# A two-layer graph network on one core: all heads scaled by ScalarE, the last list decode spread out, weights loaded earlier

## The chip, the core and the metric

The kernel runs on one core of one Trainium2 chip. The metric is the device time of one execution in microseconds. Three runs of the kernel before took 671.46, 673.04 and 673.52 us; the median is 673.04 us. One more execution was profiled: 674.27 us, of which the profile's span, from the first to the last instruction, is 672.6 us.

## The reference, cut to what matters

```python
x, adj: 4096 x 512 floats, 4096 x 4096 ints (about 4 ones in a row)
# layer 0: graph attention, 8 heads of 64, W: (8, 512, 64), a: (8, 128)
Wh = einsum('nf,hfo->hno', x, W)
e  = leaky_relu(f1[:, :, None] + f2[:, None, :], 0.2)     # f1, f2: Wh against the halves of a
attn = softmax(where(adj > 0, e, -9e15), axis=-1)
x  = layernorm(x + concat_heads(attn @ Wh))
# layer 1: mean of the neighbours and the node itself
agg = (adj > 0) @ x / max(deg, 1)
y  = relu(concat([x @ W_self + b_self, agg @ W_nb + b_nb]) @ W_comb + b_comb)
out = layernorm(x + y)
```

## The kernel before, in words

The rows are handled in 32 blocks of 128 (`NB = 32`). There are three stages. The order of instructions on each engine is the order in which the program issues them (`tc.manual_schedule()`); no scheduler moves them. Waits are added where data or a buffer require them.

**Stage 1, reading adj.** For each block two halves of 128x2048 ints are loaded by SP's DMA queue (`load_adj`, L413, four buffers `at`), turned to bf16 by ScalarE with a row sum (`mask_adj`, L419, three buffers `ab`), folded by TensorE into keys (`fold_adj`, L437), and the largest keys are taken by VectorE (`max_keys`, L452). Beside it TensorE computes Wh (`node_half`, L367), which goes to a table `t0` in DRAM. After every fourth block, `decode` turns the keys of four blocks into neighbour lists. It is a generator: each `next` runs one piece on VectorE (sometimes with a small matmul), 16 pieces for four blocks. Pieces 4 to 7 each search one block's list; pieces 9 and 10 are empty; pieces 11 to 14 build selection matrices; 15 has the matmuls L517; 16 fills `own`.

**Hand-over.** After the last block, the weights of layer 1's neighbour half are loaded (`load_fold`, `wr` and `wc`, L276 and L277, 1 MB each on SP's queue) and multiplied together on TensorE (`fold_weights`, a generator of 16 pieces: four chunks, each with transposes L293, a ScalarE copy L294, four matmuls L305 and a ScalarE copy L309). GpSimd starts the gathers: each block of layer 0 needs five indirect DMAs (`gather`, L612) of table rows. The second gather buffer lies where the adj buffers were (`ap_cm.__exit__`), so block 1's gathers wait until the last `mask_adj` has read its buffer.

**Stage 2, attention.** A software pipeline over steps i = -3 to 33. In step i, in this order:

- TensorE: `a_shared(i+1)` (L696), `a_z(i-1)` (L744), transposes of block i (L346)
- VectorE: `a_weights(i+3)` (L645), `a_weigh(i+2)` (L662), `a_recip(i+1)` (L704), `a_first`, `a_own_sum`, `a_adds(i+2)` (L670 to L686), the last part of `a_scale(i+1)` (L715), then one list piece (`some(lists)`), then `a_moments(i+1)` (L722), in some steps a bias piece (`fold_bias`, L324)
- ScalarE: `root(i)` (L730 to L736) and `norm(i)` (L739), `a_scale(i+1)` (L712), `a_exp(i+3)` (L652, L653), `a_owners(i+4)` (L639), the copy of z (L748), the copy of xT (L352)
- GpSimd: five gathers for block i+6, as soon as `a_shared(i+1)` frees the buffer (five buffers, `GA = 5`)

`a_scale` multiplies the eight heads' sums in PSUM by the reciprocals: `HA = 6` heads as six ScalarE instructions of 128x64 and the last two as one VectorE instruction of 128x128. `root(i)` needs the result of `a_moments(i)`, and `a_moments(i+1)` needs all of `a_scale(i+1)`.

The last decode (blocks 28 to 31) runs its pieces in steps 0 to 15, one in each; `late_lists` (five pieces, L555 to L597, for rows that layer 1 gathers late) follows in steps 17 to 21; bias pieces run in steps 2 to 5 and 16 to 19; `sum_bias` (L332, L333) in step 20; step 7 loads 2 MB of weights on SP's queue.

**Stage 3, layer 1.** For each block TensorE does `g_shared` (L783) and `g_self` (L776); GpSimd gathers five sets of rows per block from table `t1`, which `a_z` filled; the result goes out.

Of the kernel before, what the change touches and what calls it, by code (L numbers as in the profile page):

```python
# [36 lines left out]
OP = mybir.AluOpType  # L37
# [3 lines left out]
P = 128  # L41
# [71 lines left out]
def listed_layers(  # L113
# [15 lines left out]
    nc = tc.nc  # L129
    N, FIN = x.shape  # L130
    H, _, D = w0.shape
    NB = N // P
    FB = FIN // P
    HD = H * D
    HH = HD // 2
# [12 lines left out]
    FIRST = (0, 1, 3)  # L148
    EARLY = NB - 3
    LB = NB - 2  # L150
    HA = 6

    t0 = tc.dram_tile([N + 2, TW], F32, name="t0")
    t1 = tc.dram_tile([N + 2, HD], F32, name="t1")
# [111 lines left out]
    def pads(wp):  # L266
        pad = wp.tile([P, FW], F32, name="row", bufs=2)
        nc.vector.memset(pad[0:1, 0:H], -BIG)
        nc.vector.memset(pad[0:1, H:FW], 0.0)
        nc.scalar.dma_start(t0[0:1, :], pad[0:1, 0:TW])  # L270
        nc.scalar.dma_start(t1[0:1, :], pad[0:1, H:TW])
        nc.scalar.dma_start(t1[1:2, :], pad[0:1, H:TW])


    def load_fold(k, w, wr, wc):
        nc.sync.dma_start(wr, w.rearrange("(c p) o -> p c o", p=P))  # L276
        nc.sync.dma_start(  # L277
            wc, w_comb[k * HD : (k + 1) * HD, :].rearrange("(c p) o -> p c o", p=P)
        )
        return wr, wc  # L280
# [9 lines left out]
    def turned(wr, c, wT, bank):  # L290
        tp = ps.tile([P, FB, P], F32, name=bank)
        for d in range(FB):
            nc.tensor.transpose(tp[:, d, :], wr[:, c, ts(d, P)], ident)  # L293
        nc.scalar.copy(wT, tp.rearrange("p c r -> p (c r)"))  # L294
        return wT.rearrange("p (c r) -> p c r", c=FB)

    def fold_weights(loaded, place, bank):

        wr, wc = loaded
        wT = turned(wr, 0, place(0), bank)  # L300
        for c in range(FB):
            nxt = turned(wr, c + 1, place(c + 1), bank) if c + 1 < FB else None
            mp = ps.tile([P, HD], F32, name="mp")
            for d in range(FB):
                nc.tensor.matmul(  # L305
                    mp, lhsT=wT[:, d, :], rhs=wc[:, d, :], start=(d == 0), stop=(d == FB - 1)
                )
                if d == FB - 1:
                    nc.scalar.copy(wr[:, c, :], mp)  # L309
                yield  # L310
            wT = nxt
# [24 lines left out]
    def load_x(b, eng=nc.sync):  # L336
        if b < NB:
            eng.dma_start(xs[:, b, :], x[ts(b, P), :])
# [69 lines left out]
    def load_adj(b, ap):  # L408

        for h in range(NH):  # L410
            at = loads[b, h] = ap.tile([P, NG // NH, SC], I32, name="at", bufs=4)
            r = b * P + h * (P // NH)
            nc.sync.dma_start(  # L413
                at, adj[r : r + P // NH, :].rearrange("(j r) (s c) -> (r s) j c", r=RG, s=SEG)
            )

    def mask_adj(b, h):
        ab = masks[b, h] = bp.tile([P, NG // NH, SC], BF16, name="ab", bufs=3)
        nc.scalar.activation(  # L419
            ab, loads.pop((b, h)), AF.Relu, accum_out=asum[:, b, h : h + 1]  # L420
        )
# [189 lines left out]
    def rows_of(out, table, at):  # L611
        nc.gpsimd.indirect_dma_start(  # L612
            out=out, out_offset=None, in_=table,
            in_offset=bass.IndirectOffsetOnAxis(ap=at, axis=0),
        )
# [5 lines left out]
    def gather(table, b, g, at=None):  # L621
        for k in range(KS):
            rows_of(
                g[:, k, 0 : table.shape[1]], table, (idx if at is None else at)[:, b, k : k + 1]
            )
        return g
# [8 lines left out]
    G0, OWN, E, RD, Y, NM, MV, RS = ({} for _ in range(8))  # L635

    def a_owners(b, wp):
        OWN[b] = wp.tile([P, KH, P], F32, name="own", bufs=4)
        nc.scalar.copy(  # L639
            OWN[b].rearrange("p k c -> p (k c)"), own[:, b].rearrange("p k c -> p (k c)")  # L640
        )
# [63 lines left out]

    def a_scale(b):

        for h in range(HA):
            a, q = divmod(h, H // 2)
            o = a * HD + (1 - a) * H + q * D  # L710
            s = NM[b][:, o : o + D]
            nc.scalar.mul(s, s, RD[b][:, h : h + 1])  # L712
        o = HD + HH - (H - HA) * D
        s = NM[b][:, o : HD + HH].rearrange("p (h d) -> p h d", d=D)
        nc.vector.tensor_tensor(  # L715
            s, s, RD[b][:, HA:].unsqueeze(2).to_broadcast([P, H - HA, D]), OP.mult
        )

    def a_moments(b, wp):
        Y[b] = wp.tile([P, HD], F32, name="y", bufs=2)  # L720
# [95 lines left out]
    def some(todo):  # L816
        for p in todo:
            next(p, None)

    wp = ctx.enter_context(tc.tile_pool(name="work", bufs=1))  # L820
    fc_cm = tc.tile_pool(name="foldc", bufs=1, side="right")
    fc = fc_cm.__enter__()
    fp_cm = tc.tile_pool(name="fold", bufs=1, side="right")
    fp = fp_cm.__enter__()

    def weight(pool, name):
        return pool.tile([P, FB, HD], F32, name=name)
# [101 lines left out]
    for b in range(LB - 1):  # L929
        for k in range(1 + (b in AHEAD)):  # L930
            load_x(w + k + XL)
        load_adj(b + 2, ap)
        if b == 4:
            pads(wp)
        for k in range(2):
            some(lists)
        for k in range(1 + (b in AHEAD)):
            nxt = transposed(w + 1, wp, sums)
            if k == 0 and b in (22, 23, 24):
                transposed(EARLY + b - 22, wp, sums, True)  # L940
            if k == 0:
                key_bank(b + 1)
                for h in range(NH):
                    mask_adj(b + 1, h)
            node_block(w, xT, None if k else b)
            w, xT = w + 1, nxt
        for k in range(2):
            some(lists)
        if b == 25:
            pieces = mean_row(w_sb, sums, xa)  # L950
        if b >= 25:
            next(pieces, None)
        if b % G == G - 1:
            lists = [decode(b + 1 - G, dp, on_own)]
    m2 = weight(fp, "wr")
    loaded = load_fold(1, w_nb, m2, weight(fc, "wc"))
    load_adj(LB + 1, ap)
    row = node_block(w, xT, keep=True)
    key_bank(LB)
    mask_adj(LB, 0)  # L960
    store(w, row)
    fold_adj(LB - 1, dp)
    max_keys(LB - 1)
# [3 lines left out]
    def place(c):  # L967
        return wp.tile([P, FW], F32, name="row", bufs=2)[:, 0:FIN]
# [4 lines left out]
    def pieces(n, todo):  # L973
        for k in range(n):
            next(todo)

    gps = [gather_buffer(0)]
    G0[0] = gather(t0, 0, gps[0])
    mask_adj(LB, 1)
    key_bank(LB + 1)  # L980
    m2s = fold_weights(loaded, place2, "pw")
    pieces(1, m2s)
    fold_adj(LB, dp)
    max_keys(LB)
    pieces(3, m2s)
    mask_adj(LB + 1, 0)
    for k in range(4):
        some(lists)
    pieces(3, m2s)
    mask_adj(LB + 1, 1)  # L990
    pieces(1, m2s)
    ap_cm.__exit__(None, None, None)
    gps.append(gather_buffer(1))
    G0[1] = gather(t0, 1, gps[1])
# [14 lines left out]
                t[:, a * HD : (a + 1) * HD], lhsT=triu, rhs=cols, start=True, stop=True  # L1009
            )  # L1010
    G0[2] = gather(t0, 2, gps[2])
    a_owners(0, wp)
    lists = [chain(lists[0], decode(NB - G, dp, on_last))]


    def on(b):
        return 0 <= b < NB
# [3 lines left out]
    for i in range(-3, NB + 2):  # L1021
        if on(i + 1):
            a_shared(i + 1)
        if on(i + 1 + GA):
            G0[i + 1 + GA] = gather(t0, i + 1 + GA, gps[(i + 1 + GA) % GA])
        elif on(i + GA - NB - 1) and i + GA - NB - 1 < GA:
            b = i + GA - NB - 1
            G1[b] = gather_early(b, gps[(NB + b) % GA])
        if on(i + 3):
            a_weights(i + 3, wq)  # L1030
        if on(i + 2):
            a_weigh(i + 2, slice(K0, KS))
        if on(i + 1):
            a_recip(i + 1, wq)
        if on(i + 2):
            a_first(i + 2)
            a_weigh(i + 2, slice(1, K0))
            a_own_sum(i + 2)
            a_adds(i + 2)
        if on(i):  # L1040
            root(i, xs[:, i, :])
            norm(i, xs[:, i, :])
        if on(i + 1):
            a_scale(i + 1)
        if i > -3:
            some(lists)
        if i == 16:
            lists = [late_lists(dp, last.rearrange("p g (a k) -> p (g a) k", a=2))]
        if on(i + 1):
            a_moments(i + 1, wq)  # L1050
        if on(i + 3):
            a_exp(i + 3)
        pieces({-3: 2, -2: 2}.get(i, 0), m2s)
        if on(i + 4) or i == -3:
            a_owners(i + 4, wp)
        if on(i - 1):
            a_z(i - 1, XT.pop(i - 1), m2, wp)
        if on(i):
            XT[i] = transposed(i, wp)
            store_xT(i, XT[i])  # L1060
        if 2 <= i < 6:
            next(biased)
        if i == 7:
            loaded = load_fold(0, w_self, m1, weight(fc, "wc"))
        if 16 <= i < 20:
            if i == 16:
                biased = fold_bias(loaded, bcol[:, 0:FB])
            next(biased)
        if i == 20:
            sum_bias()  # L1070
# [481 lines left out]
```

## Time and profile before

| what | us |
|---|---|
| median of three runs | 673.04 |
| the profiled execution, time | 674.27 |
| its span | 672.6 |
| TensorE busy (share of the span) | 597.7 (89%) |
| VectorE busy | 472.4 (70%) |
| ScalarE busy | 476.6 (71%) |
| GpSimd busy | 352.6 (52%) |
| stage 1, until the last row of t0 is stored | 0 to 220 |
| hand-over, until root(0) starts | 220 to 254.4 |
| stage 2, root(0) to root(31) | 254.4 to 462.2 |
| stage 3, from the first L783 | 472.2 to 672.6 |

In a timeline line the columns are the start and the duration in us, the engine, the line of the kernel, the operation with its tiles and shapes, how many were merged, and in brackets how long the engine stood idle before it and what ended that. In a table of stages, each line is one stretch of time: its bounds, its length, then the busy time and the number of instructions of PE, PEld, VectorE (DVE), ScalarE (ACT) and GpSimd (POOL), the granted TensorE clock, the DMA share and GB/s.

### The profile page before, as it was taken

To read this page: it belongs to the slowest core of one execution; us is meant where nothing else is said; L and a number is where in the kernel's file an instruction comes from. 1 tells how busy PE (TensorE), PEld (TensorE's weight loads), DVE (VectorE), ACT (ScalarE), POOL (GpSimd) and SP (SyncE) were. 2 spreads that over 40 slices of the span, in tenths; PEclk is the share of its full clock that TensorE was granted. 3 is DMA by queue.
4 is the path that set the end of the run, shared out by engine and by line. 5 is a ranking of instruction groups with operands and counts; after the bars stand their busy time and mean duration, and the time that the engine had idled before them with its cause. 6 is when DMAs were issued, how large, how long until landed. Compare 5 with 4: busy or idle time off the path is not lost.

```text
span 672.6 us, 8973 instructions
## 1 busy us (share of the span) xinstructions
PE 597.7 (89%) x2229; PEld 346.2 (51%) x2230; DVE 472.4 (70%) x1293; ACT 476.6 (71%) x1249; POOL 352.6 (52%) x474
## 2 busy tenths in 40 slices
PE   4788989898798958978899889999899999999993
PEld 2566767666665335545455456564444444444441
DVE  6236867868786569999899999992315665666663
ACT  2688888788886326888788778996326677677664
POOL 5111111111112577777777756547777677777760
PEclk9988989989999876999999999999999999999997
DMA  8999999999999577989998987859879898999991
GB/s 247 408 408 407 409 407 408 407 410 408 402 405 405 182 210 229 290 287 298 391 283 299 281 260 224 297 183 295 284 221 307 255 329 310 307 317 308 312 310 67
DMA packets 92037, 209.63 MB, mean 312 GB/s; under 512 B 13694, under 2 KB 13702, under 8 KB 91978
## 3 DMA queue, kind: packets, MB, share of 16 engines
q1 hardware_dynamic: 63024, 114.05, 45.3%
q0 software_dynamic: 28624, 94.39, 43.9%
q10 hardware_dynamic: 330, 0.54, 0.3%
q8 instruction: 20, 0.33, 0.2%
q14 instruction: 39, 0.32, 0.2%
HBM read 175.25 MB, written 33.69 MB: 311 GB/s over the span
## 4 chain that ended last, share of the span: by engine, by line
PE 51%; DMA 26%; DVE 8%; ACT 7%; issue 3%; POOL 3%; SPq 1%; ACTq 0%; DVEq 0%; POOLq 0%
DMA at<-in_adj_dram 15%; PE nm L776 8%; PE pw L776 8%; PE pw L744 8%; DMA g<-t,idx 8%; PE pw L367 6%; PE num L696 5%; PE nm L783 4%; PE pw L783 4%; ACT ab L419 4%; PE tp L305 3%; POOL g L612 3%; DMA wc<-in_L_gnn_W_comb_dram 2%; DVE g L662 2%; PE tp L346 2%
## 5 line engine op out<-in xcount | busy, mean ns | idle before, releaser
L612 POOL DMA_INDIRECT g<-t,idx x290 | 276.1, 952 | 106.9 <-issue 37.5
L419 ACT ACTIVATE ab<-at 128x2048 bf16<-128x2048 int32 x64 | 122.5, 1915 | 32.4 <-DMA at<-in_adj_dram 26.7
L367 PE MATMUL pw<-w_sb,xT 128*128 128x264 f32 x512 | 135.2, 411 | 8.1 <-issue 3.8
L744 PE MATMUL pw<-wr,xT 128*128 128x512 f32 x256 | 116.5, 598 | 3.2 <-ACT xT L352 3.2
L367 PEld LDWEIGHTS pw<-w_sb,xT 128*128 128x128 f32 x512 | 97.2, 199 | 37.0 <-issue 7.2
L374 POOL COPY lst<-row 128x8 f32<-128x8 f32 x32 | 6.5, 203 | 165.0 <-DVE row L371 152.2
L696 PE MATMUL num<-g,own 128*128 128x264 f32 (+1 forms) x256 | 71.7, 429 | 18.7 <-DVE num L686 10.2
L662 DVE TENSOR_TENSOR g<-g,ew 128x1024 f32<-128x1024 f32 x64 | 77.4, 1210 | 0.0
L744 PEld LDWEIGHTS pw<-wr,xT 128*128 128x128 f32 x256 | 48.5, 192 | 52.2 <-issue 46.2
L696 PEld LDWEIGHTS num<-g,own 128*128 128x128 f32 x256 | 51.2, 210 | 32.5 <-DVE num L686 12.8
L712 ACT ACTIVATE num<-num,rd 128x64 f32<-128x64 f32 x192 | 54.7, 285 | 10.0 <-DVE rd L704 4.8
L776 PE MATMUL nm<-m,xT 128*128 128x512 f32 x128 | 57.5, 592 | 0.0
L776 PE MATMUL pw<-m,xT 128*128 128x512 f32 x128 | 57.5, 592 | 0.0
L371 DVE COPY row<-pw 128x264 f32<-128x264 f32 x64 | 27.3, 426 | 33.4 <-PE pw L367 21.4
L799 DVE SCALAR_TENSOR_TENSOR sm<-y,lst,nm 128x512 f32<-128x512 f32 x16 | 12.1, 754 | 52.4 <-PE nm L793 28.7
L346 PEld LDWEIGHTS tp<-ident,xs 128*128 128x128 f32 x256 | 32.2, 148 | 29.5 <-issue 11.5
L686 DVE TENSOR_TENSOR num<-num,g 128x512 f32<-128x512 f32 x64 | 44.7, 699 | 2.2
L346 PE MATMUL tp<-ident,xs 128*128 128x128 f32 x256 | 41.1, 285 | 5.7 <-DVE tl L570 2.5
L776 PEld LDWEIGHTS nm<-m,xT 128*128 128x128 f32 x128 | 24.3, 190 | 30.6 <-issue 30.6
L776 PEld LDWEIGHTS pw<-m,xT 128*128 128x128 f32 x128 | 24.3, 190 | 30.6 <-issue 30.1
L612 POOL DMA_INDIRECT g<-t,idxe x30 | 28.5, 949 | 19.6 <-DVE num L670 9.1
L730 ACT ACTIVATE xs<-y,ln_sum 128x512 f32<-128x512 f32 x32 | 23.3, 728 | 17.1 <-DVE y L722 17.1
(219 smaller groups left out, 981.1 us busy)
## 6 DMA issues: line engine op xcount, KB each, us to landing
at<-in_adj_dram SPq DMA_DIRECT2D x64, 1024.0 KB, 10.7
xt<-xT SPq DMA_DIRECT2D x32, 256.0 KB, 4.3
t<-row SPq DMA_DIRECT2D x32, 256.0 KB, 3.9
xT<-xt SPq DMA_DIRECT2D x32, 256.0 KB, 5.1
out_dram<-row SPq DMA_DIRECT2D x32, 256.0 KB, 5.5
t<-row POOLq DMA_DIRECT2D x31, 260.0 KB, 5.5
xs<-in_x_dram SPq DMA_DIRECT2D x31, 256.0 KB, 10.7
g<-t,idx POOLq DMA_INDIRECT x290, 5.0
```

The source lines that it names most:

```text
L346: nc.tensor.transpose(tp[:, c, :], xs[:, b, ts(c, P)], ident)
L367: nc.tensor.matmul(pw, lhsT=xT[:, c, :], rhs=w_sb[:, c, k * HW : (k + 1) * HW], start=(c == 0), stop=(c == FB - 1),)
L371: nc.vector.tensor_copy(row[:, k * HW : (k + 1) * HW], pw)
L419: nc.scalar.activation(ab, loads.pop((b, h)), AF.Relu, accum_out=asum[:, b, h : h + 1])
L612: nc.gpsimd.indirect_dma_start(out=out, out_offset=None, in_=table, in_offset=bass.IndirectOffsetOnAxis(ap=at, axis=0),)
L662: nc.vector.tensor_tensor(gv, gv, E[b][:, sl].unsqueeze(3).to_broadcast([P, sl.stop - sl.start, H, D]), OP.mult,)
L686: nc.vector.tensor_add(halves_of(NM[b]), halves_of(NM[b]), G0[b][:, k, H:TW].rearrange("p (a c) -> p a c", a=2),)
L696: nc.tensor.matmul(NM[b][:, a * HD : a * HD + r.stop - r.start], lhsT=OWN[b][:, k, :], rhs=G0[b][:, K0 + k, r], start=False, stop=(k == KH ...
L712: nc.scalar.mul(s, s, RD[b][:, h : h + 1])
L744: nc.tensor.matmul(pz, lhsT=xT[:, c, :], rhs=m2[:, c, :], start=(c == 0), stop=(c == FB - 1))
L776: nc.tensor.matmul(NM[b], lhsT=xT[:, c, :], rhs=m1[:, c, :], start=False, stop=(c == FB - 1), skip_group_check=True,)
L783: nc.tensor.matmul(NM[b], lhsT=OWN[b][:, k, :], rhs=g[:, K0 + k, 0:HD], start=False, stop=(k == KH - 1), skip_group_check=True,)
```

## The change

`a_scale` does all eight heads on ScalarE; the VectorE instruction L715 and `HA` go. The last decode's pieces run in three of four steps (0, 1, 2, 4, 5, 6, 8, ... 18, 20) and `late_lists` follows in steps 22, 24, 25, 26 and 28. The two loads of `load_fold(1, ...)` are issued ahead of block 30's adj loads instead of ahead of block 31's. In the hand-over, the pieces of `fold_weights` come ahead of the masks that they used to follow: two chunks are done around the masks of block 30 and the first mask of block 31, and the last four pieces all come in step -3. The first `a_owners` moves into step -3, behind `a_exp(0)`.

```diff
-    HA = 6
@@ a_scale
-        for h in range(HA):
+        for h in range(H):
             a, q = divmod(h, H // 2)
             o = a * HD + (1 - a) * H + q * D
             s = NM[b][:, o : o + D]
             nc.scalar.mul(s, s, RD[b][:, h : h + 1])
-        o = HD + HH - (H - HA) * D
-        s = NM[b][:, o : HD + HH].rearrange("p (h d) -> p h d", d=D)
-        nc.vector.tensor_tensor(
-            s, s, RD[b][:, HA:].unsqueeze(2).to_broadcast([P, H - HA, D]), OP.mult
-        )
@@ stage 1
+        if b == LB - 2:
+            m2 = weight(fp, "wr")
+            loaded = load_fold(1, w_nb, m2, weight(fc, "wc"))
         load_adj(b + 2, ap)
...
-    m2 = weight(fp, "wr")
-    loaded = load_fold(1, w_nb, m2, weight(fc, "wc"))
     load_adj(LB + 1, ap)
     row = node_block(w, xT, keep=True)
     key_bank(LB)
-    mask_adj(LB, 0)
     store(w, row)
@@ hand-over
     G0[0] = gather(t0, 0, gps[0])
+    m2s = fold_weights(loaded, place2, "pw")
+    pieces(1, m2s)
+    mask_adj(LB, 0)
+    pieces(3, m2s)
     mask_adj(LB, 1)
     key_bank(LB + 1)
-    m2s = fold_weights(loaded, place2, "pw")
+    pieces(3, m2s)
+    mask_adj(LB + 1, 0)
     pieces(1, m2s)
     fold_adj(LB, dp)
     max_keys(LB)
-    pieces(3, m2s)
-    mask_adj(LB + 1, 0)
     for k in range(4):
         some(lists)
-    pieces(3, m2s)
     mask_adj(LB + 1, 1)
-    pieces(1, m2s)
     ap_cm.__exit__(None, None, None)
...
-    a_owners(0, wp)
@@ stage 2, step i
-        if i > -3:
+        if -3 < i < 0 or i % 4 < 3 and i >= 0:
             some(lists)
-        if i == 16:
+        if i == 21:
             lists = [late_lists(dp, last.rearrange("p g (a k) -> p (g a) k", a=2))]
...
-        pieces({-3: 2, -2: 2}.get(i, 0), m2s)
-        if on(i + 4) or i == -3:
+        if i == -3:
+            a_owners(0, wp)
+        if on(i + 4):
             a_owners(i + 4, wp)
+        if i == -3:
+            pieces(4, m2s)
```

## The prediction

> **What bounds the kernel now.** I first read the table of stages, for who is busy where in stage 2. Columns: stretch, length, busy PE, PEld, VectorE, ScalarE, GpSimd, clock, DMA share, GB/s.
>
> ```profile
> 280.00:300.00 20.00, 16.48 (x55) 9.88 (x56) 19.52 (x50) 15.63 (x49) 15.40 (x16) 1.00 0.90 289
> 360.00:380.00 20.00, 18.22 (x63) 10.59 (x62) 19.52 (x45) 16.60 (x54) 15.12 (x17) 1.00 0.91 300
> 420.00:440.00 20.00, 20.00 (x73) 12.15 (x72) 19.49 (x44) 19.05 (x63) 10.03 (x11) 1.00 0.77 257
> ```
>
> Until about 400 VectorE is full and ScalarE has a fifth free. At 420 to 440 PE, VectorE and ScalarE are all full. GpSimd looks half free, but early it issues 16 gathers in 20 us, one per 1.25 us.
>
> Next, the timeline of ScalarE over one late step, root(26) to root(27), and of VectorE: a step with a list piece, then one without.
>
> ```profile
> 428.05 0.74 ACT L730 ACTIVATE xs<-y,ln_sum 128x512 f32<-128x512 f32 x1
> 430.61 1.87 ACT L712 ACTIVATE num<-num,rd 128x64 f32<-128x64 f32 x6
> 432.41 0.20 ACT L652 ACTIVATE ew<-e 128x40 f32<-128x40 f32 x1
> 433.89 0.74 ACT L730 ACTIVATE xs<-y,ln_sum 128x512 f32<-128x512 f32 x1
> ```
> ```profile
> 302.30 0.29 DVE L715 TENSOR_TENSOR num<-num,rd 128x128 f32<-128x128 f32 x1
> 303.31 0.67 DVE L722 SCALAR_TENSOR_TENSOR y<-num,xs 128x512 f32<-128x512 f32 x1
> ...
> 427.74 0.19 DVE L645 TENSOR_TENSOR e<-g,f1s 128x40 f32<-128x40 f32 x1
> 432.60 0.29 DVE L715 TENSOR_TENSOR num<-num,rd 128x128 f32<-128x128 f32 x1
> 432.93 0.69 DVE L722 SCALAR_TENSOR_TENSOR y<-num,xs 128x512 f32<-128x512 f32 x1
> 433.54 0.20 DVE L645 TENSOR_TENSOR e<-g,f1s 128x40 f32<-128x40 f32 x1
> ```
>
> No line carries an idle bracket. ScalarE needs 433.89 - 428.05 = 5.84 us a step, six scales in 432.41 - 430.61 = 1.80 us, 0.30 each. VectorE needs 5.80, and a list piece lengthens that. PE repeats L696 at 426.95 and 432.75: 5.80 too.
>
> The waits of ScalarE from 254 to 463 tell what its free time was:
>
> ```profile
> ACT xs L730 <- DVE y L722: 17.1, 16, 2.8
> ACT row L748 <- PE pw L744: 4.8, 5, 2.3
> ACT row L748 <- PE num L696: 2.3, 1, 2.3
> ```
>
> Mostly it waited for VectorE's moments. The hand-over, last: ScalarE, PE, GpSimd and VectorE, each from its timeline.
>
> ```profile
> 225.45 0.58 ACT L309 COPY wr<-tp 128x512 f32<-128x512 f32 x1 [7.40 <-PE tp L305]
> 225.93 1.91 ACT L419 ACTIVATE ab<-at 128x2048 bf16<-128x2048 int32 x1
> 228.30 1.92 ACT L419 ACTIVATE ab<-at 128x2048 bf16<-128x2048 int32 x1
> ```
> ```profile
> 218.28 2.05 PE L305 MATMUL tp<-wc,last 128*128 128x512 f32 x2 [2.20 <-DMA wc<-in_L_gnn_W_comb_dram]
> ```
> ```profile
> 225.51 0.95 POOL L612 DMA_INDIRECT g<-t,idx  x1 [0.30 <-issue]
> 230.58 0.94 POOL L612 DMA_INDIRECT g<-t,idx  x1 [4.12 <-ACT ab L419]
> ```
> ```profile
> 240.08 0.20 DVE L645 TENSOR_TENSOR e<-g,f1s 128x40 f32<-128x40 f32 x1 [4.95 <-DMA g<-t,idx]
> ```
>
> `wc` lands at 218; PE multiplies; ScalarE stands 7.40 us behind PE with both masks of block 31 queued behind; block 1's gathers wait 4.12 us for the last mask, and VectorE 4.95 us for those gathers. That chain starts stage 2.
>
> **What the Trainium skill says.** "ScalarE: Activation LUTs", What ACT_TABLE_LOAD costs: an ACTIVATE costs 186 ns plus 0.833 ns per element plus about 93 ns per pointer operand, and neighbours overlap by some 93 ns; for 64 elements and one pointer that is 332 ns. The trace has 285 ns each and 0.30 us from one to the next, so no overlap in this chain; I use 0.30. "TensorE: Matmul & The Clock Gate", What's actually happening: after an idle window of some 3.4 us the clock halves until a busy window has passed. The trace agrees: clock 0.50 at 250 to 260, where L696 takes 3.81 us, and 1.92 later. "DMA: Bandwidth & Descriptors", Issuing engines are not separate DMA queues: all queues share 16 engines. Here they are full until 220 (share 1.05), so an earlier load only reorders landings.
>
> **Hand-over.** The 2 MB go ahead of block 30's adj. At 408 GB/s that is 5.1 us: block 30 lands at about 215.5 and 218 rather than 210.5 and 213; block 31 still lands by about 221, when the DMA share falls. `wr` and `wc` are there when PE ends the node matmuls at 214. Then on ScalarE: two L294 copies to 215.8; mask(30,0) (2.0) to 217.8; chunk 0's four matmuls (3.43) end at 218.8, L309 to 219.3; mask(30,1) to 221.3; L429 and L294 to 222.3; mask(31,0) to 224.2; L309 to 224.7; mask(31,1) to 226.7. Its buffer was mask(30,0)'s, freed by `fold_adj(30)` near 223.5, so that wait is covered. Block 0's gathers end at 226.5. Block 1's start at about 226.9: **3.7 us gained**, and G0[1], which ends VectorE's 4.95, lands 3.7 earlier. If PE falls to half clock here, the masks end at 229.8 and 0.7 is left. What hides the three extra copies and the casts of `a_owners`: VectorE waits for G0[1] anyway. Step -1 loses L715 ahead of moments(0): another 0.2. Start of stage 2: **-3.9**.
>
> **Eight scales on ScalarE.** 2 x 0.30 = 0.60 per step on an engine that has none to give late: 5.84 becomes 6.43. Over 31 steps: steps 0 to 27 give 28 x 6.43 = 180.2, less 0.5 for a missing z copy in step 0; steps 28 to 30, which drop casts and exps, 5.54, 5.37 and 5.39 plus 0.60 each, 18.1; `sum_bias`'s copy 0.5. That is 198.3 with no idle, against 207.8 measured (254.44 to 462.23) with the old load of 179.7 and so 28.1 idle. ScalarE becomes the bound; its idle decides.
>
> **VectorE.** L715 to L722 without a piece is 0.33: the step falls to 5.47. A piece costs its L715-to-L722 distance less 0.20: the search at 302.30 is 0.81; by the same reading pieces 1 to 3 are 1.05, 0.66, 0.86, piece 8 1.47, piece 11 1.17, 12 to 14 0.78, 15 1.48, 16 1.13, late pieces 1.31, 1.69, 1.31, 1.43, 1.53; a bias piece 0.66. By the new places, steps over 6.43 are: 2, 4, 5 (6.99, 6.94, 6.94), 9 (6.94), 13 (6.64), 16 to 18 (6.91, 6.91, 7.61), 20 (6.60), 22, 24 to 26, 28 (6.78, 7.16, 6.78, 6.90, 7.00). Scales end 2.56 + 2.39 = 4.95 after root, moments (0.77) by 5.7: in light steps VectorE gets up to 0.7 ahead, which swallows lone heavy steps (9, 13, 20, 22). Left: 0.6 in step 2, 0.7 in 4 and 5, 1.4 in 16 to 18, 0.8 in 24 to 26, 0.2 in 28: **3.7**. Matmuls of pieces 11 and 15 and of the late lists move with them to PE, which at 5.80 has room.
>
> **Other idle of ScalarE.** Steps 0 and 1 are paced by PE at half clock: 14.5 us stays, 2.1 over ScalarE's 12.4. Step 10 waited 3.1 (2.3, 0.8) for stores behind the 2 MB of step 7; longer steps give these more time, so between 0 and 3.1: 1.5. `sum_bias`: 1.2 as before. Sum 2.1 + 3.7 + 1.5 + 1.2 = 8.5; stage 2 takes 206.8, **-1.0**. GpSimd at 5 x 1.25 = 6.26 a step stays below 6.43. Stage 3 is PE without gaps from 509 and moves as a whole; its early gathers come sooner too.
>
> **Sum.** -3.9 - 1.0 = -4.9: 674.27 becomes 669.4 in a profiled execution; that one lies 1.2 above the median, so on the scale of the runs 673.04 - 4.9 = **668.1**. In general the shift is ScalarE's idle less 13.4.
>
> **Rivals.** (1) The hand-over yields 0.7 instead of 3.9, start and all, because PE is at half clock while ScalarE waits on its copies: -1.7, 671.3. For it: half clock at 218 to 224 before. Against: that followed PE's wait for `wc`, which goes. (2) Slower: the stalls that VectorE's bound used to hide now add to ScalarE's full queue. Place: steps 10, 16 to 28. Price: all waits of before other than on moments, 10.9, plus the heavy steps' whole excess, 6.2 to 6.7 with nothing swallowed: idle 17.1 or more, +3.7, 676.7. It decides from idle 13.4 on. For it: a wait on PE or DMA can't be made up on a full engine; against: half of the 10.9 arose where late lists, bias and `sum_bias` fell together, which the change pulls apart.
>
> **Chances.** Changes under 0.3% (2.0 us) can't be told from none. Forecast, gain over 2: 0.63. Rival 1 and idle of 11.4 to 15.4: 0.20. Rival 2: 0.17. Range: below, idle of 5 (-8.4) gives 664.6; above, it takes in rival 1 and the start of rival 2, 675.0.
>
> **What would show it.** L712 in groups of eight, 2.4 us, steps of 6.43 without brackets on ScalarE in the last third (if 5.8, the price is wrong); the wait on moments down from 17.1 to about 4; block 1's gathers at 227 (at 230: rival 1); root(0) near 250.5, root(31) near 457.4. If root(31) is past 464, rival 2.

## The result and the profile after

The changed kernel takes 672.52 us in the median of 12 runs (670.55 to 675.67); the kernel before, run beside it, 671.15 us in the median of 12 (669.11 to 673.52). The ratio is 1.001, with a 95% interval of 0.9986 to 1.0034: no difference that can be told, where 4.9 us less were forecast. In microseconds the interval reaches from -0.9 to +2.3, so the forecast gain is excluded.

The two profiled executions say something else: 674.27 us before, 671.37 after, 2.9 less. The first lies 3.1 above the median of the 12 runs of its kernel, the second 1.1 below that of its own. That gap is the main subject of what follows.

I read the profile after in the order of the prediction. The table of stages, columns as before:

```profile
280.00:300.00 20.00, 16.87 (x59) 9.99 (x58) 19.48 (x48) 17.71 (x60) 15.18 (x16) 1.00 0.92 295
360.00:380.00 20.00, 18.77 (x73) 11.06 (x73) 19.52 (x43) 18.66 (x61) 15.43 (x16) 1.00 0.93 285
420.00:440.00 20.00, 17.63 (x61) 9.96 (x61) 19.18 (x44) 18.57 (x62) 6.73 (x8) 1.00 0.55 180
```

ScalarE gained 2 us of work per 20 in the first two stretches; VectorE still looks full. Busy shares no longer tell which is the bound. The groups on the page show the moved work, with count, busy time and mean ns: 256 scales where there were 192, at 286 ns each where there were 285.

```profile
L711 ACT ACTIVATE num<-num,rd 128x64 f32<-128x64 f32 x256 | 73.1, 286 | 10.2 <-DVE rd L703 2.9
```

ScalarE's timeline, from root(26) to root(27) in the late third:

```profile
428.01 0.72 ACT L724 ACTIVATE xs<-y,ln_sum 128x512 f32<-128x512 f32 x1 [0.18 <-DVE y L716]
...
430.56 2.51 ACT L711 ACTIVATE num<-num,rd 128x64 f32<-128x64 f32 x8
432.99 0.20 ACT L651 ACTIVATE ew<-e 128x40 f32<-128x40 f32 x1
...
434.77 0.72 ACT L724 ACTIVATE xs<-y,ln_sum 128x512 f32<-128x512 f32 x1 [0.18 <-DVE y L716]
```

Eight scales take 432.99 - 430.56 = 2.43 us. This step has a late list and takes 6.76; steps without one take 6.48 where they took 5.84. The waits of ScalarE over stage 2 (254 to 463), in us, times and the longest:

```profile
ACT xs L724 <- DVE y L716: 3.4, 7, 1.4
ACT row L742 <- DMA t<-row: 2.4, 1, 2.4
ACT brow L332 <- PE tp L331: 1.2, 1, 1.2
ACT xT L351 <- DMA xt<-xT: 0.7, 1, 0.7
```

The wait for VectorE's moments fell from 17.1 to 3.4. The window is that of the prediction and opens 3.6 us behind the changed kernel's root(0), so it leaves out the wait ahead of that; from 250 to 460 the sum is 5.3. The same view of VectorE shows the other side, the kernel before first, the changed kernel second:

```profile
DVE num L715 <- ACT num L712: 5.1, 2, 3.1
```
```profile
DVE y L716 <- ACT num L711: 11.0, 9, 4.1
```

VectorE now waits for ScalarE nine times where it waited twice, and longer than ScalarE waits for it: the bound has changed hands, though not in every step. Last the hand-over, on ScalarE, GpSimd and VectorE:

```profile
219.01 0.59 ACT L308 COPY wr<-tp 128x512 f32<-128x512 f32 x1 [1.40 <-PE tp L304]
...
224.76 1.93 ACT L418 ACTIVATE ab<-at 128x2048 bf16<-128x2048 int32 x1
```
```profile
227.04 0.96 POOL L611 DMA_INDIRECT g<-t,idx  x1 [0.76 <-ACT ab L418]
```
```profile
236.34 0.20 DVE L644 TENSOR_TENSOR e<-g,f1s 128x40 f32<-128x40 f32 x1 [1.76 <-DMA g<-t,idx]
```

The 7.40 us behind TensorE became 1.40, the 4.12 of GpSimd 0.76, the 4.95 of VectorE 1.76. In this execution the hand-over is where the prediction put it: block 1's gathers at 227.04, root(0) at 250.40. Root(31) is not: 459.49 instead of 457.4.

The span can be cut in five at marks read from the timelines: the first gather of block 0 (called S from here on), root(0), root(21), root(31), the end. From root(31) to the end it takes 210.2 to 210.5 us in every kernel here but one (211.2 in e10). All profiled kernels in one table, worked out from the starts of those instructions:

```
kernel, its profile               S       S to    root(0)   root(21)
                                        root(0)   to (21)    to (31)
before                         220.39    34.05    147.56     60.23
before, another execution      220.43    33.38    148.89     59.92
after                          220.21    30.19    144.88     64.21
e1 hand-over alone             222.53    30.42    148.59     59.87
e2 eight scales alone          220.10    30.41    147.06     65.65
e3 hand-over + spread, six     222.31    29.66    145.44     63.90
e4 eight in piece steps only   221.30    30.18    144.24     63.48
e5 before + filled wait        221.99    29.70    146.39     59.07
e6 e4 + split load             220.65    30.27    139.16     63.18
e8 e6 + three fillings         222.45    30.58    139.33     63.12
e9 e6 with the old hand-over   220.60    32.13    139.91     63.20
e10 after + split load         220.46    29.31    140.96     64.20
e11 before + split load        220.51    32.94    146.05     60.02
e12 e6 + one filling           220.98    29.12    140.36     63.22
```

Each line is a single execution, and the table shows how far such a one can be trusted. Before, its other execution, e1 and e5 have the same instructions from root(0) on, and root(0) to root(31) takes 207.79, 208.81, 208.46 and 205.46 us in them.

### The profile page after: what moved, and what is told of

It is laid out like the page before. It is cut to its first block, busy times and chain, and to the rows that moved or that the text cites. A ratio compares the mean times of both kernels' runs of the same rounds, so it can differ in the third digit from the quotient of the medians.

```text
span 669.7 us, 9002 instructions
## 1 busy us (share of the span) xinstructions
PE 591.0 (88%) x2229; PEld 338.8 (51%) x2230; DVE 466.2 (70%) x1261; ACT 494.2 (74%) x1313; POOL 354.2 (53%) x474
## 4 chain that ended last, share of the span: by engine, by line
PE 42%; DMA 32%; DVE 12%; ACT 9%; issue 3%; SPq 1%; POOL 0%; ACTq 0%; DVEq 0%; POOLq 0%
DMA at<-in_adj_dram 18%; DMA g<-t,idx 10%; PE nm L770 8%; PE pw L770 8%; PE nm L777 4%; PE tp L304 4%; PE pw L366 4%; PE pw L777 4%; DVE g L661 4%; ACT ab L418 4%; PE pw L738 3%; DMA xt<-xT 2%; DVE num L685 2%; PE num L695 2%; ACT num L711 2%
## 5 line engine op out<-in xcount | busy, mean ns | idle before, releaser
L366 PE MATMUL pw<-w_sb,xT 128*128 128x264 f32 x512 | 130.4, 400 | 6.9 <-issue 3.8
L738 PE MATMUL pw<-wr,xT 128*128 128x512 f32 x256 | 119.1, 609 | 6.5 <-ACT xT L351 6.3
L366 PEld LDWEIGHTS pw<-w_sb,xT 128*128 128x128 f32 x512 | 94.6, 194 | 33.8 <-issue 9.0
L695 PE MATMUL num<-g,own 128*128 128x264 f32 (+1 forms) x256 | 66.3, 404 | 17.6 <-DVE num L685 10.3
L711 ACT ACTIVATE num<-num,rd 128x64 f32<-128x64 f32 x256 | 73.1, 286 | 10.2 <-DVE rd L703 2.9
L695 PEld LDWEIGHTS num<-g,own 128*128 128x128 f32 x256 | 47.7, 196 | 29.2 <-DVE num L685 14.4
L370 DVE COPY row<-pw 128x264 f32<-128x264 f32 x64 | 27.3, 427 | 31.9 <-PE pw L366 23.9
L770 PEld LDWEIGHTS pw<-m,xT 128*128 128x128 f32 x128 | 24.3, 190 | 30.6 <-issue 30.4
L770 PEld LDWEIGHTS nm<-m,xT 128*128 128x128 f32 x128 | 24.3, 190 | 30.6 <-issue 30.6
L777 PE MATMUL nm<-g,own 128*128 128x512 f32 x64 | 30.2, 594 | 1.3 <-ACT nm L761 1.3
```

Of the source, the lines that this page charges most:

```text
L366: nc.tensor.matmul(pw, lhsT=xT[:, c, :], rhs=w_sb[:, c, k * HW : (k + 1) * HW], start=(c == 0), stop=(c == FB - 1),)
L370: nc.vector.tensor_copy(row[:, k * HW : (k + 1) * HW], pw)
L695: nc.tensor.matmul(NM[b][:, a * HD : a * HD + r.stop - r.start], lhsT=OWN[b][:, k, :], rhs=G0[b][:, K0 + k, r], start=False, stop=(k == KH ...
L738: nc.tensor.matmul(pz, lhsT=xT[:, c, :], rhs=m2[:, c, :], start=(c == 0), stop=(c == FB - 1))
L770: nc.tensor.matmul(NM[b], lhsT=xT[:, c, :], rhs=m1[:, c, :], start=False, stop=(c == FB - 1), skip_group_check=True,)
L777: nc.tensor.matmul(NM[b], lhsT=OWN[b][:, k, :], rhs=g[:, K0 + k, 0:HD], start=False, stop=(k == KH - 1), skip_group_check=True,)
```

## The experiments

**The parts one by one.** My theory was still that of the prediction, corrected by the trace: the hand-over gives 4 us, the scales and the spread take some back. The first kernel has the hand-over part of the diff and nothing else.

```diff
 (the kernel before, with these parts of the change only)
+        if b == LB - 2:
+            m2 = weight(fp, "wr")
+            loaded = load_fold(1, w_nb, m2, weight(fc, "wc"))
...
+        if i == -3:
+            a_owners(0, wp)
...
```

> The kernel before with the hand-over part alone (loads of wr and wc ahead of block 30's adj, products ahead of the masks, a_owners(0) and the last four pieces in step -3); six heads on ScalarE, lists in the old steps. My theory: root(0) starts at about 250.5 rather than 254.4, and since stage 2 is as before (207.8 us from root(0) to root(31), step 5.84) the whole gain of about 4 us reaches the end: ratio 0.994. Rival A (the gain at root(0) is eaten in stage 2 by waits on DMA or gathers): root(0) at 250.5, but stage 2 at 210 or more and a ratio of 0.998 to 1.000. Rival B (the profiled execution of before was late in this place by chance, the gain is not real): root(0) is early here too, but the runs stand at 1.000.

Measured: 672.26 us (14 runs, 667.66 to 673.52) against 670.94; ratio 0.9998, 0.9974 to 1.0023. Here and below the ratio and its 95% interval are those on record; they are not the quotient of the two medians, which would be 1.002 here and also lies in the interval. Root(0) was at 252.95, not 250.5, because S came 2.1 later, and the median shows no gain: rival B's reading, and the first blow to my theory. The second kernel holds only the scales.

```diff
-    HA = 6
+    HA = 8
...
-        nc.vector.tensor_tensor(
-            s, s, RD[b][:, HA:].unsqueeze(2).to_broadcast([P, H - HA, D]), OP.mult
-        )
```

> The kernel before with eight heads on ScalarE alone; hand-over and list steps as before. My theory: root(0) at about 254; ScalarE's step is 6.48 us where nothing holds it, pieces in every one of steps 0 to 15 make VectorE's steps longer than that (5.47 plus 0.6 to 1.5 with two more in steps 2 to 5 and 16 to 19), so that less is swallowed than in the changed kernel, and the steps from 22 to 28 lose 0.64 each: stage 2 takes 209 to 212 us, ratio 1.003 to 1.006. Rival (VectorE's relief of 0.33 a step pays in the early half what ScalarE loses in the late half): stage 2 at 207 to 208, ratio 1.000.

Measured: 678.05 us (7 runs, 675.36 to 680.06); ratio 1.0102, 1.0067 to 1.0138. Worse than I expected, 7 us slower; the profile, taken on the fastest of the seven, shows 4.9 of them in stage 2, and the rest is not explained. Root(21) to root(31) took 65.65 against 60.23: 5.4 us, eight steps or so by 0.64. The early steps gave only 0.5 back (147.06 against 147.56), since a step now takes the longer of 6.48 on ScalarE and VectorE's with its piece. VectorE's waits of stage 2 show who is the bound:

```profile
DVE y L717 <- ACT num L712: 15.3, 13, 4.6
```

And it gave a surprise: with the old hand-over, S to root(0) took 30.41 here, as short as the new one. Third, the changed kernel with six scales:

```diff
 (the changed kernel)
+    HA = 6
-        for h in range(H):
+        for h in range(HA):
...
+        nc.vector.tensor_tensor(
+            s, s, RD[b][:, HA:].unsqueeze(2).to_broadcast([P, H - HA, D]), OP.mult
+        )
```

> The changed kernel with HA = 6 again: hand-over and spread lists, the last two heads on VectorE. My theory: ScalarE's step is 5.84 again and VectorE's 5.80 plus its pieces, of which the sum over the stage is the same as before; the gain is the hand-over's alone, root(31) about 4 us earlier than before, ratio 0.994. Rival A (spreading the pieces into the late third, where TensorE has no room at 5.80 a step, costs by itself): stage 2 at 210 us or more and a ratio of 0.998 to 1.001, as the changed kernel. If ratio 0.994, the eight scales are what took the hand-over's gain back.

Measured: 671.56 us (14 runs); ratio 1.0006, 0.9978 to 1.0034. Not 0.994, so the eight scales are not what ate the gain. It is the ratio of rival A, with stage 2 at 209.34, just short of its 210. Spreading alone (e1 to e3) shortens the early part by 3.2 and lengthens the late one by 4.0: with six scales the late list pieces are only moved. With eight (e2 to after) it saves 2.2 early and 1.4 late. Fourth, eight scales only where VectorE has a piece:

```diff
-        for h in range(H):
+        i = b - 1
+        ha = H if i < 0 or i % 4 < 3 and i < 29 else H - 2
+        for h in range(ha):
...
```

> The changed kernel with eight heads on ScalarE only in steps in which VectorE has a list piece (three of four up to step 28), and six in the others (3, 7, 11, 15, 19, 23, 27, 29 to 31). My theory: ten steps fall from 6.48 to 5.84, 6.4 us, but VectorE gets no further ahead in them, so that the excess of heavy steps is swallowed less (up to 2.5 us back): stage 2 at 204 to 206, ratio 0.993 to 0.996. Rival (light steps only let ScalarE wait for VectorE's backlog): stage 2 at 208 to 209, ratio 0.999 to 1.002, as the changed kernel.

Measured: 669.34 us (22 runs); ratio 0.9978, 0.996 to 0.9997. A small gain, less than I expected: stage 2 took 207.72, 1.4 under the changed kernel in one profile each. Light steps did fall to 5.83, but the steps behind them grew (step 28 from 6.36 to 7.01, step 24 from 6.54 to 7.21), as the rival says: VectorE no longer gets ahead in the light ones.

**Where the hand-over's gain came from.** Why is the old hand-over 34.05 once and 30.41 once? TensorE's timelines say it, the kernel with eight scales alone (e2) first, then another execution of the kernel before (e7), for which this was expected:

> The kernel before once more, for a second look at its own hand-over. Theory (half clock by chance): from the first gather to root(0) it takes 30.4 us if L305 runs at full clock after wc (six matmuls in 2.8 us), or 34 if at half (4.2 us), and all else is within 0.5 us. Stage 2 at 207.5 to 208.7. Rival: 34 us with L305 at full clock.

```profile
218.03 1.10 PE L305 MATMUL tp<-wc,last 128*128 128x512 f32 x2 [2.20 <-DMA wc<-in_L_gnn_W_comb_dram]
219.06 0.62 PE L437 MATMUL key<-ab,fold 128*32 128x512 bf16 x8
219.60 2.84 PE L305 MATMUL tp<-wc,last 128*128 128x512 f32 x6
```
```profile
218.67 1.10 PE L305 MATMUL tp<-wc,last 128*128 128x512 f32 x2 [2.37 <-DMA wc<-in_L_gnn_W_comb_dram]
219.70 1.03 PE L437 MATMUL key<-ab,fold 128*32 128x512 bf16 x8
220.66 4.08 PE L305 MATMUL tp<-wc,last 128*128 128x512 f32 x6
```

It took 674.62 us in one run, S to root(0) 33.38. The same six products behind the same wait of 2.2 to 2.4 us take 2.84 us or 4.08. The granted clock from 221 to 223 is 1.00 in the first and 0.50 in the second, so most of the six ran at half clock there. In the first profile of before even the two ahead of them took 2.05, and the six 4.19:

```profile
221.23 4.19 PE L305 MATMUL tp<-wc,last 128*128 128x512 f32 x6
```

From the first of these products to the end of the six it is 4.4 us in e2, 6.0 to 6.1 in e7, e9 and e11, and 7.1 in before. So 2.7 of the 3.6 us between before and e2 are this clock. The rest lies between block 1's gathers and root(0), where all the profiles vary from 22.4 to 23.9 us, with either order. The Trainium skill, "TensorE: Matmul & The Clock Gate", What's actually happening, says that the activity window is free-running and that the moment of the switch depends on where in it the work falls; that agrees with what is seen, though no run here shows the window itself. The prediction reckoned with an idle window of some 3.4 us, and these waits are shorter: the half clock came behind a single wait of 2.2 us (ahead of which stood 1.06 us of matmuls and another wait of 0.9), and at 245 in the kernel before behind one of 2.95. If the wait sets it off, filling the wait must make the old order as fast as the new:

```diff
             mp = ps.tile([P, HD], F32, name="mp")
+            if c == 0 and bank == "pw":
+                for _ in range(8):
+                    nc.tensor.matmul(mp, lhsT=triu, rhs=cols, start=True, stop=True)
```

> The kernel before with one addition: eight matmuls of 128x512 bf16 (0.26 us each at full clock) into mp, overwritten afterwards, in TensorE's queue where it stood 2.20 us waiting for wc. What the traces showed so far: with the old hand-over, from the first gather of block 0 to root(0) took 34.05 us in the profile of before, where the products behind that wait ran at half clock, and 30.41 us in the profile with only eight scales added, where they ran at full clock; with the new hand-over 29.7 to 30.4. Theory (revised): the 3.7 to 4 us that the hand-over part seemed to gain were TensorE's half clock in one execution, which starts or does not start behind a 2 us wait by chance. With the wait filled the span from the first gather to root(0) is 30.2 to 30.6 here, L309's first copy waits under 5 us, and the median moves by 0 to -1.5 us (the 3.6 us times how often it happens): ratio 0.998 to 1.000. Rival (the new order itself shortens the chain, and the eight scales run was the odd one): 34 us here, ratio 1.000 or above.

```profile
216.82 1.89 PE L306 MATMUL tp<-cols,triu 128*128 128x512 bf16 x8
219.21 1.13 PE L308 MATMUL tp<-wc,last 128*128 128x512 f32 x2 [0.50 <-ACT last L294]
220.27 0.61 PE L440 MATMUL key<-ab,fold 128*32 128x512 bf16 x8
220.81 2.84 PE L308 MATMUL tp<-wc,last 128*128 128x512 f32 x6
```

Measured: S to root(0) 29.70, under the expected 30.2: old order, new time. One of the five profiles of the old order without the filling is as fast (e2), so this one execution does not prove that the filling keeps the clock. The median moved little: 671.13 us (14 runs), ratio 0.9994, 0.9973 to 1.0016.

S itself varies in the same way. In e1 it came 2.1 later than before, in e3 1.9, in e5 1.6. Some 1.7 us of each arose where the node matmuls behind a 2.02 us wait near 182 slowed down: 3.32 us (e1), 2.58 (e3, with 2.71 in the next eight) and 3.10 (e5) for what took 2.05 before, in code that all these kernels share. Before first, then e1:

```profile
183.28 2.05 PE L367 MATMUL pw<-w_sb,xT 128*128 128x264 f32 x8 [2.02 <-DVE sums L356]
183.81 3.32 PE L367 MATMUL pw<-w_sb,xT 128*128 128x264 f32 x8 [2.02 <-DVE sums L356]
```

**The stall of step 10.** In the changed kernel step 10, from root(10) to root(11), takes 9.77 us where its neighbours take 6.5. SP's queue and ScalarE's timeline show why:

```profile
305.38 0.49 SPq L275 DMA_DIRECT2D m<-in_L_gnn_W_self_dram  x1
305.97 0.94 SPq L276 DMA_DIRECT2D wc<-in_L_gnn_W_comb_dram  x1
311.01 0.34 SPq L743 DMA_DIRECT2D t<-row  x1
```
```profile
325.84 0.59 ACT L742 COPY row<-pw 128x512 f32<-128x512 f32 x1 [2.39 <-DMA t<-row]
327.12 0.59 ACT L351 COPY xT<-tp 128x512 f32<-128x512 f32 x1 [0.69 <-DMA xt<-xT]
```

The store issued at 311.01, behind 2 MB of loads, released its buffer only at 325.84, 14.8 us later; the store of xT issued next to it, at 311.50, is recorded with 15.5 us from issue to landing. The median of the stores from 303 to 330, from issue to landing, is 4.4. Two buffers of `row` bridge two steps, 13 us. So the loads were cut up, first on e4:

```diff
-            loaded = load_fold(0, w_self, m1, weight(fc, "wc"))
+            loaded = (m1, weight(fc, "wc"))
+        if 7 <= i < 15:
+            k, c = divmod(i - 7, FB)
+            src = (w_self, w_comb[0:HD, :])[k].rearrange("(c p) o -> p c o", p=P)
+            nc.sync.dma_start(loaded[k][:, c, :], src[:, c, :])
```

> The kernel with eight scales only in piece steps (hand-over, spread), and the 2 MB that step 7 loads at once now loaded as eight DMAs of 256 KB, one in each of steps 7 to 14. Theory: step 10 (9.8 us in both the changed kernel and this one's base) loses its 2.2 to 2.4 us wait for the store of row and 0.7 us for xT, which lay behind the 2 MB: step 10 at 6.5 to 7, root(31) about 2.5 to 3 us earlier, ratio to before 0.994. Rival A (the store itself is slow because the gathers fill the engines at that time, share 0.9): step 10 stays at 9 or more. Rival B (the small loads each delay a store a little in eight steps): step 10 is short but steps 8 to 15 are longer by 0.3 each, nothing gained: ratio 0.998.

Its ScalarE at the end of step 10:

```profile
322.73 0.58 ACT L750 COPY row<-pw 128x512 f32<-128x512 f32 x1
323.20 0.59 ACT L351 COPY xT<-tp 128x512 f32<-128x512 f32 x1
323.68 0.74 ACT L732 ACTIVATE xs<-y,ln_sum 128x512 f32<-128x512 f32 x1
```

No bracket is left: step 10 takes 6.46. Measured: 665.82 us (6 runs, 665.35 to 667.79); ratio 0.992, 0.9895 to 0.9945. Both rivals fall: step 10 is short, and steps 8, 9 and 11 to 15 are at most 0.03 longer than in e4. The Trainium skill says in "DMA: Bandwidth & Descriptors", Issuing engines are not separate DMA queues, that transfers of all issuers share 16 engines and interleave; here it mattered which of one issuer's transfers had been put first.

The same edit on the changed kernel and on the kernel before:

> The changed kernel with one edit: the 2 MB of step 7 as eight loads of 256 KB in steps 7 to 14. Theory: step 10 goes from 9.77 to 6.5 us, all else stays: 3.2 us less than the changed kernel's 672.5, so 669.3, ratio to before 0.9965. Rival (the time shows up as heavier steps elsewhere, since VectorE used the stall to catch up): 1 us or less, ratio 1.000.

Measured: 668.31 us (11 runs); ratio 0.9938, 0.9913 to 0.9962, better than expected; step 10 6.48, and no other step grew by it.

> The kernel before with the same edit alone. Theory: step 10 goes from 9.2 to 9.7 us to 7.1 (VectorE then is the bound there with its list pieces), 2.1 to 2.6 us less: 668.5, ratio 0.9965. If VectorE's pieces had caught up in the stall, half of that: ratio 0.998. If nothing, VectorE is the bound there in any case: 1.000.

Measured: 670.06 us (22 runs, beside 672.23 for before); ratio 0.9965, 0.9946 to 0.9985; step 10 6.80. With the edit on both, the change brings the time to 0.9938 / 0.9965 = 0.9973, 1.8 us less, and the two medians, taken side by side, differ by the same 1.8; without the edit it is 1.001. In the profiles the edit took 3.3 us from step 10 where ScalarE is the bound (9.77 to 6.48), and 2.4 to 2.9 from that of the kernel before (9.19 and 9.73 to 6.80).

**The clock in stage 1, and the hand-over once more.** Fillings of seven matmuls were put ahead of `max_keys` in three steps of stage 1:

```diff
             fold_adj(between, dp)
+            if between in (22, 23, 24):
+                t = ps.tile([P, HD], F32, name="sm", bufs=2)
+                for _ in range(7):
+                    nc.tensor.matmul(t, lhsT=triu, rhs=cols, start=True, stop=True)
```

> As the kernel with the split load, and in stage 1 the three steps in which TensorE waits for a sum on VectorE (2.02 us at 181 to 183 before) filled with seven matmuls of 128x512 bf16 each into a spare bank. Theory: the half-clock phase behind the last of these waits, which shifted the rest by 1.7 and 0.9 us in two profiles of four with the new hand-over, is gone: node halves there at 2.05 us; the median is 0.5 to 1 us under that of the split load alone, ratio to before 0.992 to 0.993. Rival (the phase is not set off by this wait, or the filling delays the node matmuls): same as the split load, or up to 1 us above.

```profile
167.62 1.68 PE L915 MATMUL sm<-cols,triu 128*128 128x512 bf16 x7
169.14 1.94 PE L366 MATMUL pw<-w_sb,xT 128*128 128x264 f32 x8
...
183.19 1.69 PE L915 MATMUL sm<-cols,triu 128*128 128x512 bf16 x7
185.29 2.05 PE L366 MATMUL pw<-w_sb,xT 128*128 128x264 f32 x8 [0.41 <-DVE sums L355]
```

Measured: 667.14 us (6 runs), ratio 0.9935, 0.9911 to 0.9959; S at 222.45, 1.8 later than in e6. A miss of mine: only the last of the three stood in a wait. The other two lay where TensorE went from the fold straight to the node matmuls and pushed these back, as the rival says: the first by 1.5 us. With the filling in the last one only (`between == 24`):

> The kernel with split load, mixed scales, spread lists and new hand-over, with seven filling matmuls only in the one step of stage 1 in which TensorE did wait (2.02 us for the sum on VectorE, near 181). In the run with three fillings two lay where TensorE had no wait and pushed the node matmuls back by some 1.5 us. Theory: the single filling keeps the clock full and costs nothing: first gather at 220.2 to 220.7 in the profile, median as with the split load alone or up to 0.5 us less, 665.3 to 665.8, ratio 0.9915. Rival (the clock falls here whether or not the wait is filled, or the filling costs time itself): first gather at 221.3 or later, median 666.5 or more.

Measured: 665.33 us (6 runs, 664.25 to 666.19), the fastest here; ratio 0.9878, 0.9839 to 0.9917 (the medians' quotient is 0.9897). S was at 220.98, 0.3 later than in e6, and these 0.3 were there before the filling. Whether the filling did anything against e6 can't be told. Beside it, on the same chip, ran the same stage 2 with the hand-over of before:

> The kernel with the split load, mixed scales and spread lists, but with the hand-over of before: tells what the new hand-over is worth where the rest is steady. As predicted at first: root(0) 3.7 to 4 us later in every execution, median near 669.7, ratio 0.998. Revised theory (the old order costs 3 to 3.6 us only in executions in which TensorE falls to half clock behind the wait for wc, and 0.2 otherwise): median 666 to 668.5, single runs spread over more than 3 us; in the profile first gather to root(0) is 30.2 to 30.6 with six L305 in 2.8 us, or 33 to 34 with them in over 4 us, nothing else. If the median is 665.8 with a narrow spread, the half clock is rare outside the profiles and the part is worth nothing.

Measured: 668.24 us (10 runs, 667.0 to 669.79); ratio 0.9934, 0.9906 to 0.9962; six L305 in 3.73 us, S to root(0) 32.13. Every run of e12 is faster than every run of this one; 2.9 us lie between the medians, for the new hand-over and the filling together, and S to root(0) differs by 3.0. The median is within what the revised theory expected; the six L305 lie between its two cases.

## Why the prediction was wrong in its gain, and right in its range

The measured 672.52 lies in the stated range, 664.6 to 675.0, which was wide enough for rival 1 and the start of rival 2. The forecast in the middle of it, 4.9 us less, did not come. That the absolute miss is no larger is partly luck: the 673.04 from which the forecast started is the median of three runs, 1.9 above the later median of twelve.

**Hand-over, -3.9: the step that failed.** The prediction put "3.7 us gained" at block 1's gathers and -3.9 at root(0). Its chain for the new order came true to half a microsecond. What failed is the other side of the difference: it took 230.58, the start of block 1's gathers before, as what the old order costs. In that execution TensorE ran at half clock behind the wait for `wc`. The prediction knew of this half clock: rival 1 names it at 218 to 224. But it weighed only whether the new order might suffer from it, not what the old order takes without it; that the old order pays for it in every execution was taken from a single profile. Without it block 1's gathers start 7.5 us behind S (e2) or 6.84 (e5), against 6.83 in the changed kernel. In five profiles with the old order, filled wait apart, S to root(0) is 30.41 to 34.05, 32.6 in the mean; in eight with the new 29.1 to 30.6, mean 30.0. So the part is worth 0.2 to 3.9 in the profiles, 2.6 in the mean, and most of the difference is the clock. Over runs, on the kernel before, it is worth nothing that can be told (e1; filling the wait instead, in e5, shows nothing either). On the kernel with the split load, e9 against e12, it is up to 2.9. Why the runs show it there and not here is open. GpSimd also bounds it: its five gathers of block 0 take until 225.33 + 1.25 = 226.58 in the changed kernel, 6.4 us behind S, so that no more than half a microsecond of the 6.83 is left to be had.

**Stage 2, -1.0: measured +0.7 to +1.5, in one profile.** 209.09 us against 207.79 in the profile, or 208.35 as the mean of three profiles with that stage 2 (before, its other execution, e1); with e5 as a fourth the mean is 207.6. The mechanism held: ScalarE became the bound, VectorE's heavy steps were swallowed in part, the late third gave time back. Two terms were mis-sized. A ScalarE step is 6.48, not 6.43, 1.5 us over 31 steps: each scale added 0.32, not 0.30. Step 10 kept 3.3 us of idle where "between 0 and 3.1: 1.5" was taken: 1.8. Against that, the other idle together came out some 1 us smaller than the 7.0 set. The argument that longer steps give stores more time had the size wrong: 0.64 more in each of two steps against a landing that took 14.8 us.

**The base.** The sum was made against the profiled 674.27 and moved to the median as if the execution were only slower all over. It stood 3.1 above the later median, and part of those microseconds was in the wait that was to be removed. A shift against one execution counts its bad luck as gain.

**Rivals.** Rival 1's event (half clock in the new order while ScalarE waits) did not happen in any profile; that its time, 671.3, came out nearest is luck. Idle beyond ScalarE's predicted load of 198.3 was 10.8 us, between the forecast's 8.5 and the 13.4 from which rival 2 decides. Rival 2 named the right price: waits on DMA now add to a full queue. Its place held for step 10 only; root(31) stayed at 459.49, under its 464.

**What stays open.** From the profiles the change should give -2.6 + 0.7 = -1.9 us (-1.1 with e5 in the mean of stage 2); the runs say -0.9 to +2.3. With the load split on both kernels it is -1.8, so the rest seems to sit in the stall of step 10, larger over runs than in the one profile: ratios fall by 0.7% (about 4.8 us) from after to e10, where the profiles fall by 3.3. But those ratios were not measured side by side, each has an interval half a per cent wide, and in the profiles with the stall step 10 varies from 9.1 to 10.0 us (8.0 in e5). So this is argued, not shown. Nor is it settled how often the half clock strikes in runs that are not profiled: four of five profiles of the old order have it, but e1 and e5 say that it costs the median little, while e9 against e12 leaves room for 2.9 us.

## What to carry to other kernels

Before you book a stall as gain, see whether the instructions behind it ran at their usual length: the same matmuls elsewhere in the trace are the yardstick, and a single execution at half clock makes any edit in that place look good. When work moves to another engine, the new bound inherits every wait that the old one used to hide, so look for the DMA waits on it first; here a load cut in eight gave more than the change that it was meant to support. Work moved from a full engine to a nearly full one should be moved only in the steps that need it (e12, which has one filling besides, against e10: 3.0 us in the medians, taken side by side; e4 against the changed kernel points the same way, but their intervals overlap).

## What the runs showed of the hardware

- Behind waits of 2.02 to 2.45 us the same TensorE instructions ran at full clock in some executions and partly at half in others: six 128x512 products in 2.84 us (e2) or 4.19 (before), a node half in 2.05 (before) or 3.32 (e1). At the first of these places four of five profiles slowed down, at the second three of twelve.
- With eight 128x512 bf16 matmuls in the wait, 1.89 us in all, the clock stayed full in the one execution seen (e5); that they were the reason is not shown. Seven of them where TensorE had no wait took 1.7 us of its time and moved what followed by 1.5 (e8).
- A 256 KB store issued behind 2 MB of loads of the same queue released its buffer 14.8 us later, where the stores of the same stretch take 4.4 (after) and 4.7 (e6) in the median. With the loads cut up, the wait for it was gone.
- A 128x64 scale in PSUM with a pointer operand takes 286 ns, and another two of them in a chain lengthened the step by 0.64 us, 0.32 each.
